# Half-product aggregations and moved edge weights in a graph attention layer

## The chip, the cores and the metric

The kernel runs on one core of a Trainium2 chip. It computes a whole graph network of four layers in one launch, in 32-bit floating point, with its weights in HBM and its activations in SBUF. The metric is the device time of one launch in microseconds (us); the median of three runs is what is compared.

A core has five engines with queues of their own, each of which takes its instructions in order: TensorE multiplies matrices (PE in the profile; PEld is its loading of the stationary operand), VectorE (DVE), ScalarE (ACT) and GpSimd (POOL) do elementwise work, and SyncE (SP) issues the transfers (DMAs). An engine waits for another through semaphores.

## The reference

There are 512 nodes with 768 features and 16384 edges. The change is in the graph attention of layer 0, which has eight heads in its first part and one in its second:

```
def gat_layer(x, W, a_s, a_d, b, edge_index, concat):
    h = (x @ W).reshape(n, H, C)                       # H = 8, C = 768
    alpha_s = jnp.einsum('nhc,hc->nh', h, a_s)         # score of a node as source
    alpha_d = jnp.einsum('nhc,hc->nh', h, a_d)         # and as target
    e = jax.nn.leaky_relu(alpha_s[src] + alpha_d[dst], NEG_SLOPE)
    m = jax.ops.segment_max(e, dst, num_segments=n)
    e = jnp.exp(e - m[dst])
    denom = jax.ops.segment_sum(e, dst, num_segments=n)
    alpha = e / (denom[dst] + EPS)
    out = jax.ops.segment_sum(h[src] * alpha[:, :, None], dst, num_segments=n)
    return out.reshape(n, H * C) + b

h = jax.nn.elu(gat_layer(x, W1, a_src1, a_dst1, b1, edge_list, concat=True))
out = gat_layer(h, W2, a_src2, a_dst2, b2, edge_list, concat=True)
```

So for each head i: h_i = x W1_i (512x768 by 768x768), edge weights alpha (as a dense 512x512 matrix w, target by source, since the graph is small), g_i = elu(w h_i + b), and h2 += g_i W2_i.

## The kernel before, in words

**Counts.** `edge_counts` builds a dense matrix `cnt` of how many edges lead from each source to each target, and from it `off`, which is 0 where an edge exists and 1e30 where none does (L725). The weights of a head come from the two scores of each node (`node_scores`, L796: four multiply-and-sum instructions of 128x768 for a score) in `weighing` (L737 to L763): TensorE turns the source scores into a row (L329), VectorE takes row minus `off` with its maximum (L743), three tiny steps make the negative maximum (L745 to L748), ScalarE adds the target score (L753), VectorE applies the slope of 0.2 (L754), ScalarE the exp (L755), VectorE multiplies by `cnt` and sums (L756), and scales (L763). Each of these is done for four tiles of 128 targets by 512 sources. `turned` (L783) transposes w into wT, source by target, on TensorE, 16 blocks of 128x128.

**Products.** Products of 768x768 matrices are made in seven half-products instead of eight (the Strassen-Winograd scheme). `SplitA` (L395) prepares four sums of quarters of the activations, `SplitB` (L429) four differences of quarters of the weights, on GpSimd, in place for one of them (L438 to L441: three times four instructions of 128x384 for a weight matrix). `strassen` (L498) makes a product whose output is either feature-major or token-major, and adds the half-products up on VectorE: `u2` at L551, `u3` at L554, then L555, L560 and L564. `strassen_add` (L593) makes a product that is added into a running sum; each half-product is added as it comes (`add`, for h2 at L921), so that one half-product can be added to two or three places. Within a column or row group, `first` and `second` are staged so that the second part of a group is written after the first part of the next (`staged`, L491).

**The order.** The loop at the end of the `gat0` block runs over i = 0 to 8. In step i it makes head i's products h_i (`heads`, the heads stage), then aggregates head i-1 (`aggregate`, L898: for each of six feature chunks four products of 128x128 by 128x512, then elu, and the sums for the projection on GpSimd), then makes head i's edge weights (`edge_weights`), and then projects head i-1 through W2 (`project`). The transposes of head i-1's weights are steps that a background list feeds into head i's products, one for each half-product (`tick`, L465). For head 0 the edge weights are in that list too. Instructions of such a step are pinned behind the last one of each engine (`pinned`). Beyond this a scheduler at build time sets the order in each engine's queue, so that instructions of neighbouring stages interleave a little.

**Weights from HBM.** Two buffers take turns: W1_i in one, W2_i in the other, each loaded in three pieces of 768 KB (`split_weights`). A load begins when the last product that reads the old contents of its buffer has ended, and each piece's GpSimd differences follow as it lands.

Of the kernel before, what the change touches and what calls it, by code (L numbers as in the profile page):

```python
# [18 lines left out]
P = 128  # L19
# [78 lines left out]
def kernel(ctx: ExitStack, tc: tile.TileContext, a: dict, out: bass.AP):  # L98
# [296 lines left out]
    class SplitA:  # L395


        def __init__(self, xT, eng, ready=True):
            h = KC // 2
            self.st = big_tile("sx")[:, : 4 * h * HT].rearrange("p (i k n) -> p i k n", i=4, k=h)  # L400
            self.eng = eng
            self.a11, self.a12 = xT[:, :h, :HT], xT[:, h:, :HT]
            self.a21, self.a22 = xT[:, :h, HT:], xT[:, h:, HT:]
            self.s = [None] + [self.st[:, i] for i in range(4)]
            if ready:
                self.all_sums()
# [18 lines left out]
    def ready(src):  # L425

        return SplitB(split_weights(src))

    class SplitB:  # L429


        def __init__(self, w):
            h = KC // 2
            tt = diff_tile("tw").rearrange("p (i k n) -> p i k n", i=3, k=h)
            b11, b12 = w[:, :h, :HC], w[:, :h, HC:]
            b21, b22 = w[:, h:, :HC], w[:, h:, HC:]
            for k in range(h):
                G.tensor_sub(tt[:, 0, k], b22[:, k], b12[:, k])  # L438
                G.tensor_sub(b12[:, k], b12[:, k], b11[:, k])  # L439
                G.tensor_sub(tt[:, 1, k], b22[:, k], b12[:, k])  # L440
                G.tensor_sub(tt[:, 2, k], b21[:, k], tt[:, 1, k])  # L441
            self.b11, self.b21, self.b22 = b11, b21, b22
            self.t = [None, b12, tt[:, 1], tt[:, 0], tt[:, 2]]

# [53 lines left out]
    def strassen(A, B, use, feature, then=None, extra=None, fresh=False):  # L498
# [6 lines left out]
        def product(bank, a, b, c, start, stop):  # L505
            tick()
            for k in range(KC // 2):
                if feature:
                    l, r = b[:, k, ts(c, P)], a[:, k, :]
                else:  # L510
                    l, r = a[:, k, ts(c, P)], b[:, k, :]
                T.matmul(bank, l, r, start=start and k == 0, stop=stop and k == KC // 2 - 1,  # L512
                         skip_group_check=True)
# [78 lines left out]

    def strassen_add(A, B, add, then=None):  # L593

# [42 lines left out]
        def chunk(m):  # L637
            def first():
                if m == 0:
                    plain()  # L640
                add(2 + m, 1, product(m, "z", A.s[1], B.t[1], True))
                add(m, 1, product(m, "y", A.s[2], B.t[2], True))
                add(2 + m, 1, product(m, "y", A.s[3], B.t[3], False))

            def second():
                add(m, 1, product(m, "z", A.s[4], B.b22, False))
                add(2 + m, 0, product(m, "y", A.a22, B.t[4], False))

            return first, second
# [11 lines left out]
    cnt = gone.tile([P, NT, N], FP, name="cnt")  # L661
    off = gone.tile([P, NT, N], BF, name="off")
    cnt_dram = tc.dram_tile([P, NT, N], FP, name="cnt_dram")
# [6 lines left out]
    def edge_counts(gp):  # L670
# [24 lines left out]
        for g in range(n_groups):  # L695
# [15 lines left out]
            for u in range(2):  # L711
# [6 lines left out]
                else:  # L718
# [4 lines left out]
                    G.tensor_add(low, low, r)  # L723
        for t in range(NT):
            S.activation(off[:, t, :], cnt[:, t, :], AF.Relu, bias=bigc, scale=-BIG)  # L725
        nc.sync.dma_start(cnt_dram, cnt)
# [9 lines left out]

    def weighing(w, src4, dst4, cnt, off):  # L737

        srow = row_of(src4)
        yield  # L740
        mx = tiny(NT, name="ga_mx")
        for t in range(NT):
            V.tensor_tensor_reduce(w[:, t, :], srow, off[:, t, :], 1.0, -3.0e38,  # L743
                                   ALU.subtract, ALU.max, mx[:, t : t + 1])
# [22 lines left out]

    def edge_weights(src4, dst4, gp, cnt, off):
        w = weight_tile(gp)
        for _ in weighing(w, src4, dst4, cnt, off):  # L770
            pass
        return w
# [33 lines left out]

    def last_gat(h, as_row, ad_row, gp, cnt, off, between=None):

        s4, d4 = node_scores(h, row(as_row), gp), node_scores(h, row(ad_row), gp)
        ew = edge_weights(s4, d4, gp, cnt, off)  # L810
        made = between() if between else None
        wT = by_source(ew, gp)
        token_product(by_chunk(wT), lambda s: h[:, s, :], add_to_x)
        return made
# [7 lines left out]
    def heads(i):  # L822
        B = first_two.pop(0) if first_two else head_weights(i)
        h = token_major("h")
        strassen_token(xs, B, lambda t, c, ps: S.copy(h[:, t, ts(c, HC)], ps), None,
                       None if i else n0.rest)
        flush()
        return h, node_scores(h, row(f"g0_as{i}"), gp), node_scores(h, row(f"g0_ad{i}"), gp)

    with tc.tile_pool(name="graph", bufs=1) as gp:  # L830
# [15 lines left out]
        loose.append(background[0])  # L846
        head0 = heads(0)
        drain()
# [46 lines left out]
    with tc.tile_pool(name="gat0", bufs=2) as gp:  # L895
        h2 = token_major("h2")

        def aggregate(i, h, wT, norm=None):  # L898
            gT = feature_major("gT")
            sums = SplitA(gT, G, False)  # L900
            for n, f in enumerate((0, 3, 1, 4, 2, 5)):
                ps = psum()
                for s in range(NT):
                    T.matmul(ps, h[:, s, ts(f, P)], wT[:, s, :], start=s == 0, stop=s == NT - 1)  # L904
                elu(gT[:, f, :], ps, col("g0_b1", i * KC + f))
                if norm and n < NT:
                    norm.chunk(n)
                if f >= KC // 2:
                    sums.sums(f - KC // 2)
            return sums  # L910

        def project(i, sums):
# [9 lines left out]

            strassen_add(sums, ready(a["L0_gnn_W2"][i * D : (i + 1) * D, :]), add)
            flush()
# [4 lines left out]
        def degrees():  # L929
# [9 lines left out]
            V.tensor_mul(dinv, dinv, nw)  # L939

        done = None
        for i in range(9):
            if done:
                g, hg, ew = done
                wT = gp.tile([P, NT, N], FP, tag="edge_wT", name="edge_wT", bufs=wt_bufs[0])
                if i < 8:
                    if i == 1:
                        background.append(delayed(5, weighing(ew, s4, d4, cnt, off)))
                    background.append(delayed(0 if i == 1 else 8, turned(ew, wT)))
                else:  # L950
                    for _ in turned(ew, wT):
                        pass
            if i < 8:
                h, s4, d4 = heads(i) if i else head0
                drain()
            if done:
                norm = performer_norm() if i == 8 else None
                sums = aggregate(g, hg, wT, norm)
            if i < 8:
                done = i, h, edge_weights(s4, d4, gp, cnt, off) if i else weight_tile(gp)  # L960
            else:
# [5 lines left out]
        x = load_x()  # L967
        qT = last_gat(h2, "g0_as", "g0_ad", gp, cnt, off, lambda: performer_features(ys, 0))
        add_row_to(x, row("g0_b2"))
# [1086 lines left out]
```

## Time and profile before

| | us |
|---|---|
| median of three runs (lowest to highest) | 3091.04 (3089.36 to 3091.62) |
| the profiled execution | 3090.54 |
| its span, first to last instruction | 3088.8 |
| TensorE busy | 3004.2 |
| layer 0's eight heads, from the first product of head 1 to the end of the last aggregation | 117.7 to 691.5 |
| one head in the middle: heads stage, aggregation, projection | 29.2, 20.6, 28.5 |
| TensorE's waits at the six projections from head 0 on | 1.19, then 1.10 each |

A row of the timeline reads: start in us from the span's start, duration, engine, line, operation, output and inputs with their shape and how many instructions are merged, and in brackets how long the engine had been idle before and what ended it. A 32-bit product is two matmul instructions. Matmul instructions are pipelined: the record of one of 128x384 lasts 487 ns, but they start 0.32 us apart. The rows of "stretches" give for a window its length, each engine's busy time and count, and then the granted clock of TensorE (1.00 is full), the busy share of the DMA engines and GB/s.

### The profile page before, as it was taken

The page shows a single profiled execution, that of the slowest core. Times are in us where ns is not written, and L with a number is a line of the kernel's source. Part 1 is how long each engine was busy: PE and PEld are TensorE (multiplying, and loading weights), DVE is VectorE, ACT ScalarE, POOL GpSimd, SP SyncE. Part 2 cuts the span into 40 slices and gives each one's busy share as a digit, 9 for nine tenths or more (in the row PEclk, how much of TensorE's full clock was granted, in tenths as well). Part 3 has the DMA queues.
Part 4 walks back from the last instruction along what each step waited for, and adds up shares of the span by engine and source line. Part 5 has one row for each costly group of instructions (what it writes and reads, how often), then busy time and mean ns, then how long its engine had stood idle before and what let it go on. Part 6 is the DMA issues. An engine that isn't in the chain of part 4 may idle for free.

```text
span 3088.8 us, 31610 instructions
## 1 busy us (share of the span) xinstructions
PE 3004.2 (97%) x11757; PEld 2006.4 (65%) x11757; DVE 1481.0 (48%) x3416; ACT 753.1 (24%) x1436; POOL 1430.7 (46%) x1532
## 2 busy tenths in 40 slices
PE   7999999999999999999899999999999999999989
PEld 3555555556766767765675367877777776677755
DVE  9855444555255235456766436333333335462341
ACT  7432322251352112004432213100000012221111
POOL 4344444452506553645641434455544457355610
PEclk9999999999999999999999999999999999999999
DMA  3211111222203223322112412122222223122222
GB/s 116 89 63 64 65 64 69 72 92 82 82 1 118 77 87 118 111 75 80 38 72 63 148 67 98 67 92 93 92 92 78 77 92 123 67 83 82 99 75 62
DMA packets 92691, 253.63 MB, mean 82 GB/s; under 512 B 9889, under 2 KB 14881, under 8 KB 91514
## 3 DMA queue, kind: packets, MB, share of 16 engines
q1 hardware_dynamic: 92538, 251.61, 23.5%
q8 instruction: 93, 1.52, 0.2%
q14 instruction: 60, 0.49, 0.1%
HBM read 244.23 MB, written 7.36 MB: 81 GB/s over the span
## 4 chain that ended last, share of the span: by engine, by line
PE 87%; DVE 9%; POOL 2%; ACT 1%; issue 1%; DMA 0%; SPq 0%; POOLq 0%; ACTq 0%; DVEq 0%
PE ps L512 43%; PE ps L605 23%; PE ps L904 5%; PE ps L308 4%; DVE oh L705 1%; PE ps L1112 1%; PE ps L1099 1%; PE ps L298 1%; PE ps L274 1%; PE ps L1937 1%; PE ps L1600 1%; POOL room L1458 1%; DVE edge_w L754 1%; PE ps L708 1%; DVE edge_w L743 1%
## 5 line engine op out<-in xcount | busy, mean ns | idle before, releaser
L438 POOL TENSOR_TENSOR tw<-w 128x384 f32<-128x384 f32 x246 | 247.3, 1015 | 960.0 <-DMA w<-in_L_gnn_W 341.8
L512 PE MATMUL ps<-sx,w 128*128 128x256 f32 x1188 | 317.3, 381 | 2.9 <-DVE sx L420 2.6
L512 PE MATMUL ps<-sx,tw 128*128 128x256 f32 x1188 | 290.3, 381 | 0.4
L605 PE MATMUL ps<-w,sx 128*128 128x384 f32 x720 | 256.5, 487 | 4.2 <-DVE sx L420 2.9
L440 POOL TENSOR_TENSOR tw<-w 128x384 f32<-128x384 f32 x246 | 252.2, 1032 | 9.6
L441 POOL TENSOR_TENSOR tw<-w,tw 128x384 f32<-128x384 f32 x246 | 250.4, 1025 | 10.4
L439 POOL TENSOR_TENSOR w<-w 128x384 f32<-128x384 f32 x246 | 250.8, 1028 | 8.9
L605 PE MATMUL ps<-tw,sx 128*128 128x384 f32 x720 | 250.4, 487 | 0.0
L512 PEld LDWEIGHTS ps<-sx,w 128*128 128x128 f32 x1188 | 225.6, 191 | 37.9 <-PE ps L512 2.2
L512 PEld LDWEIGHTS ps<-sx,tw 128*128 128x128 f32 x1188 | 219.9, 190 | 42.7 <-DVE st_u L551 7.2
L527 ACT COPY st_p<-ps 128x256 f32<-128x256 f32 (+1 forms) x127 | 49.9, 394 | 720.4 <-PE ps L512 681.5
L551 DVE TENSOR_TENSOR st_u<-st_p,ps 128x256 f32<-128x256 f32 (+1 forms) x127 | 57.2, 450 | 338.0 <-PE ps L512 337.9
L605 PEld LDWEIGHTS ps<-tw,sx 128*128 128x128 f32 x720 | 136.3, 190 | 94.6 <-DVE x L1821 1.2
L605 PEld LDWEIGHTS ps<-w,sx 128*128 128x128 f32 x720 | 136.6, 190 | 94.1 <-POOL tw L441 4.1
L654 DVE TENSOR_TENSOR x<-x,ps 128x384 f32<-128x384 f32 x216 | 115.2, 552 | 164.7 <-PE ps L605 163.4
L512 PE MATMUL ps<-xfT,w 128*128 128x256 f32 x720 | 176.9, 380 | 0.2
L512 PE MATMUL ps<-w,sx 128*128 128x384 f32 x456 | 169.2, 492 | 1.8 <-DVE ps L555 1.8
L904 PE MATMUL ps<-edge_wT,h 128*128 128x512 f32 x384 | 166.1, 593 | 0.0
L512 PE MATMUL ps<-tw,sx 128*128 128x384 f32 x456 | 160.4, 488 | 4.7 <-DVE st_u L551 4.2
L554 DVE TENSOR_TENSOR st_u<-st_p,ps 128x256 f32<-128x256 f32 (+1 forms) x127 | 57.2, 450 | 203.2 <-PE ps L512 203.2
L512 PEld LDWEIGHTS ps<-xfT,w 128*128 128x128 f32 x720 | 136.2, 190 | 23.9 <-issue 1.3
L605 PE MATMUL ps<-w,hid 128*128 128x384 f32 x432 | 142.9, 488 | 0.0
(485 smaller groups left out, 5067.6 us busy)
## 6 DMA issues: line engine op xcount, KB each, us to landing
w<-in_L_gnn_W SPq DMA_DIRECT2D x60, 768.0 KB, 6.8
w<-in_L_mix_fc_w SPq DMA_DIRECT2D x48, 768.0 KB, 6.2
row<-in_rows SPq DMA_DIRECT2D x39, 384.0 KB, 4.5
w<-in_L_mix_qkv_w SPq DMA_DIRECT2D x18, 768.0 KB, 5.2
w<-in_L_ffn_w SPq DMA_DIRECT2D x18, 768.0 KB, 7.1
w<-in_L_ffn_routed_gate SPq DMA_DIRECT2D x18, 768.0 KB, 6.0
w<-in_L_ffn_routed_up SPq DMA_DIRECT2D x18, 768.0 KB, 6.6
w<-in_L_ffn_routed_down SPq DMA_DIRECT2D x18, 768.0 KB, 5.7
```

The costliest lines, as they stand in the source:

```text
L308: T.matmul(ps, parts[k][:, ts(t, P)], w_of(k)[:, ts(c, HC)], start=k == 0, stop=k == n - 1)
L438: G.tensor_sub(tt[:, 0, k], b22[:, k], b12[:, k])
L439: G.tensor_sub(b12[:, k], b12[:, k], b11[:, k])
L440: G.tensor_sub(tt[:, 1, k], b22[:, k], b12[:, k])
L441: G.tensor_sub(tt[:, 2, k], b21[:, k], tt[:, 1, k])
L512: T.matmul(bank, l, r, start=start and k == 0, stop=stop and k == KC // 2 - 1, skip_group_check=True)
L527: S.copy(b["p1"], b["x"])
L551: V.tensor_add(b["u2"], b["p1r"], b["y"])
L554: V.tensor_add(u3, b["p1r"], b["y"])
L605: T.matmul(b[name], l[:, k, ts(m, P)], r[:, k, :], start=start and k == 0, stop=k == KC // 2 - 1, skip_group_check=True)
L654: V.tensor_add(x[:, t, ts(j, HC)], x[:, t, ts(j, HC)], ps)
L904: T.matmul(ps, h[:, s, ts(f, P)], wT[:, s, :], start=s == 0, stop=s == NT - 1)
```

## The change

Three things are changed, all in layer 0's graph attention.

1. The aggregation of a head is made by `strassen_feature`, in seven half-products of 256x384 quarters, in place of the plain product. For it h_{i-1} goes through `SplitB` (GpSimd, eight instructions, in place, with two small tiles and a new one, `h_diff`, for the results) and wT through `SplitA` (VectorE, four instructions of 128x512).
2. The edge weights of heads 0 to 6 become steps in the next head's products (`splitting`, which holds the differences, the weights, the transposes and the sums). The target scores are computed after the aggregation (`target_scores`), since the differences overwrite h. `off` is no longer kept: each weighing makes it anew into the weight tile, in four ScalarE instructions. Head 7's weights stay beside projection 6, and its transposes become steps there.
3. The projection's `strassen_add` gets `raw=True`: the two half-products of `A.a22` with `B.t[4]`, which need no sums of activations, come at the start, in banks of their own, and are added apart.

```diff
-        def __init__(self, xT, eng, ready=True):
-            h = KC // 2
-            self.st = big_tile("sx")[:, : 4 * h * HT].rearrange("p (i k n) -> p i k n", i=4, k=h)
+        def __init__(self, xT, eng, ready=True, st=None):
+            h = self.h = xT.shape[1] // 2
+            if st is None:
+                st = big_tile("sx")[:, : 4 * h * HT]
+            self.st = st.rearrange("p (i k n) -> p i k n", i=4, k=h)
...
-        def __init__(self, w):
-            h = KC // 2
-            tt = diff_tile("tw").rearrange("p (i k n) -> p i k n", i=3, k=h)
+        def __init__(self, w, tt=None):
+            h = w.shape[1] // 2
+            if tt is None:
+                tt = diff_tile("tw").rearrange("p (i k n) -> p i k n", i=3, k=h)
+                tt = [tt[:, i] for i in range(3)]
...
-    def strassen_add(A, B, add, then=None):
+    def strassen_add(A, B, add, then=None, raw=False):
...
                 if m == 0:
                     plain()
+                    for n in range(2 * raw):
+                        add(2 + n, 0, product(n, "p4", A.a22, B.t[4], True))
                 add(2 + m, 1, product(m, "z", A.s[1], B.t[1], True))
                 add(m, 1, product(m, "y", A.s[2], B.t[2], True))
-                add(2 + m, 1, product(m, "y", A.s[3], B.t[3], False))
+                ps = product(m, "y", A.s[3], B.t[3], False)
+                add(2 + m, 1, ps)
+                if raw:
+                    add(2 + m, 0, ps)
             def second():
                 add(m, 1, product(m, "z", A.s[4], B.b22, False))
-                add(2 + m, 0, product(m, "y", A.a22, B.t[4], False))
+                if not raw:
+                    add(2 + m, 0, product(m, "y", A.a22, B.t[4], False))
...
-        for t in range(NT):
-            S.activation(off[:, t, :], cnt[:, t, :], AF.Relu, bias=bigc, scale=-BIG)
...
-    def weighing(w, src4, dst4, cnt, off):
+    def weighing(w, src4, dst4, cnt):
         srow = row_of(src4)
+        for t in range(NT):
+            S.activation(w[:, t, :], cnt[:, t, :], AF.Relu, bias=bigc, scale=-BIG)
         yield
         mx = tiny(NT, name="ga_mx")
         for t in range(NT):
-            V.tensor_tensor_reduce(w[:, t, :], srow, off[:, t, :], 1.0, -3.0e38,
+            V.tensor_tensor_reduce(w[:, t, :], srow, w[:, t, :], 1.0, -3.0e38,
                                    ALU.subtract, ALU.max, mx[:, t : t + 1])
...
-        return h, node_scores(h, row(f"g0_as{i}"), gp), node_scores(h, row(f"g0_ad{i}"), gp)
+        return h, node_scores(h, row(f"g0_as{i}"), gp)
+
+    def target_scores(i, h):
+        return node_scores(h, row(f"g0_ad{i}"), gp)
...
+        last_sums = []
+
+        def splitting(w, wT, h, both, s4=None, d4=None):
+            tt = gp.tile([P, 2, NT // 2, HC], FP, tag="h_diff", name="h_diff", bufs=1)
+            at = len(nc.cur_bb.bb.instructions)
+            both.append(SplitB(h, [Chunks([part_tile("p1r", HC) for _ in range(2)]), tt[:, 0], tt[:, 1]]))
...
+            yield
+            if s4 is not None:
+                yield from weighing(w, s4, d4, cnt)
+                yield
+                yield
+            yield from turned(w, wT)
+            both.append(SplitA(wT, V, True, weight_tile(gp).rearrange("p t n -> p (t n)")))
+
-        def aggregate(i, h, wT, norm=None):
+        def aggregate(i, hB, wA, norm=None):
             gT = feature_major("gT")
             sums = SplitA(gT, G, False)
-            for n, f in enumerate((0, 3, 1, 4, 2, 5)):
-                ps = psum()
-                for s in range(NT):
-                    T.matmul(ps, h[:, s, ts(f, P)], wT[:, s, :], start=s == 0, stop=s == NT - 1)
-                elu(gT[:, f, :], ps, col("g0_b1", i * KC + f))
...
+            def use(c, n, j, ps):
+                f = 3 * j + c
+                elu(gT[:, f, ts(n, HT)], ps, col("g0_b1", i * KC + f))
+
+            def then(c):
+                sums.sums(c)
...
+            strassen_feature(wA, hB, use, then)
+            flush()
...
-            strassen_add(sums, ready(a["L0_gnn_W2"][i * D : (i + 1) * D, :]), add)
+            strassen_add(sums, ready(a["L0_gnn_W2"][i * D : (i + 1) * D, :]), add, None, True)
...
         for i in range(9):
...
+            if 0 < i < 8:
+                both, steps = parts_of(*done)
+                background.append(delayed(4, steps) if i == 1 else steps)
+                h, s4 = heads(i)
+            elif i == 0:
+                h, s4, d4 = head0
+            drain()
+            if i:
                 norm = performer_norm() if i == 8 else None
-                sums = aggregate(g, hg, wT, norm)
-            if i < 8:
-                done = i, h, edge_weights(s4, d4, gp, cnt, off) if i else weight_tile(gp)
+                g, sums = i - 1, aggregate(i - 1, *both, norm)
+            if 0 < i < 8:
+                d4 = pinned(lambda: target_scores(i, h))
+            if i < 7:
+                done = i, h, weight_tile(gp), s4, d4
+            elif i == 7:
+                both, steps = parts_of(i, h, edge_weights(s4, d4, gp, cnt))
+                background.append(delayed(8, steps))
             else:
                 ys, va = performer_values(norm)
```

`parts_of` makes the wT tile and calls `splitting`. In the part left out of `splitting`, the differences of h are put on GpSimd's queue behind the last sums of the aggregation before.

## The prediction

> **What bounds the kernel now.** I read the page first: the row of busy times and the chain that ended last.
>
> ```profile
> PE 3004.2 (97%) x11757; PEld 2006.4 (65%) x11757; DVE 1481.0 (48%) x3416; ACT 753.1 (24%) x1436; POOL 1430.7 (46%) x1532
> ...
> PE 87%; DVE 9%; POOL 2%; ACT 1%; issue 1%; DMA 0%; SPq 0%; POOLq 0%; ACTq 0%; DVEq 0%
> ```
>
> TensorE is the chain. A change pays by the products it removes and costs by each time TensorE has to wait. The change lies in layer 0's attention, so next I read TensorE's timeline over one head.
>
> ```profile
> 275.88 2.10 PE L512 MATMUL ps<-w,xnT 128*128 128x384 f32 x6
> ...
> 305.11 20.76 PE L904 MATMUL ps<-edge_wT,h 128*128 128x512 f32 x48
> ...
> 326.14 4.04 PE L605 MATMUL ps<-w,gT 128*128 128x384 f32 x12
> ...
> 337.73 2.20 PE L605 MATMUL ps<-w,gT 128*128 128x384 f32 x6 [1.10 <-DVE h L921]
> ...
> 354.61 2.10 PE L512 MATMUL ps<-w,xnT 128*128 128x384 f32 x6
> ```
>
> A head takes 354.61 - 275.88 = 78.73 us: 29.2 for the next head's products (heads stage), 20.6 for the aggregation, 28.5 for the projection. Its only wait is 1.10 us, where additions (L921) stand behind the edge weights on VectorE. A 384-wide matmul instruction costs 0.3225 us (six in 1.935) and a product has two, so 0.645. From two starts of 256-wide ones (761.54 - 758.95, 12 instructions) I take 0.216 us each.
>
> ```profile
> 758.95 2.75 PE L512 MATMUL ps<-sx,tw 128*128 128x256 f32 x12
> ...
> 761.54 1.03 PE L512 MATMUL ps<-yT,w 128*128 128x256 f32 x4
> ```
>
> **Aggregations.** Before: 48 instructions, 20.6 us. After: seven half-products x 3 column groups x 2 blocks x 2 = 84 instructions of 0.216, 18.1. Eight heads: -19.8 us. Added beside them: VectorE gets four sums of wT (0.6 each), 15 evacuations (0.42) and twelve half-width last steps of elu instead of six; ScalarE gets 36 half-width steps instead of 18 plus three copies; GpSimd gets eight differences of h (1.0 each). ScalarE per third: the 384- and 256-wide copies of L527 take 0.48 and 0.37, so a 256-wide step of elu is near 0.42, and 12 x 0.42 + 0.37 = 5.4 us under 6.05 us of TensorE. That is hidden, with little over. The differences of h run on GpSimd in the projection, after its sums, where it was idle (24.7 us in the row for 279.16 below). The wT sums end close to their first reader; I allow 0.3 us a head, +2.4.
>
> **Projections.** The three products without sums now give 18 products x 0.645 = 11.6 us before the first one with sums, and the last sums end near 10 us; this covers them. The waits of before go: 1.19, five of 1.10 and 0.75, -7.4. In their place the target scores (four of L796) stand between the additions that TensorE waits for. They meet GpSimd's sums, as explained next; walking the additions I get 0.7 us a head, six heads, +4.2. Two more additions each are hidden.
>
> **Edge weights as steps in the next head's products.** This decides. The old place was beside the projection, where GpSimd is mostly idle. The new place is the heads stage, where GpSimd splits the next W2.
>
> ```profile
> 279.16 0.99 POOL L438 TENSOR_TENSOR tw<-w 128x384 f32<-128x384 f32 x1 [24.74 <-DMA w<-in_L_gnn_W]
> ...
> 290.75 0.99 POOL L441 TENSOR_TENSOR tw<-w,tw 128x384 f32<-128x384 f32 x1
> ```
>
> Twelve instructions back to back, from 3.3 to 15.9 us of the stage. After the change they begin later: W2's load waits for the last reader of the old W2, which was two products before the projection's end and is now its very last product, so with the 4.9 us from release to first split seen here they begin at 5.2 us. What happens when VectorE's edge-weight steps meet them is seen once in the trace of before, at head 0, whose weights already ran in the background:
>
> ```profile
> 132.50 0.86 DVE L748 TENSOR_SCALAR ga_nm<-ga_nm 128x4 f32<-128x4 f32 x1
> ...
> 133.41 0.99 POOL L440 TENSOR_TENSOR tw<-w 128x384 f32<-128x384 f32 x1
> ...
> 134.08 2.27 DVE L754 SCALAR_TENSOR_TENSOR edge_w<-edge_w 128x512 f32<-128x512 f32 x2 [0.72 <-ACT edge_w L753]
> ...
> 134.48 1.32 POOL L441 TENSOR_TENSOR tw<-w,tw 128x384 f32<-128x384 f32 x1
> ```
>
> A four-element step takes 0.86 us instead of 0.17, ending with GpSimd's instruction; two L754 take 2.27 instead of 1.3, and GpSimd's instruction grows to 1.32. The two engines take turns, instruction by instruction, when VectorE's operands lie all in SBUF. L796 shows the same (0.95 alone, 1.74 beside GpSimd); rows with a PSUM operand (L551, L805, L743) don't change. So each L745, L748, L754, L756 pays up to 1 us, and a 512-wide one takes 1.4 instead of 0.6. L763 is seen only without GpSimd (0.42); a like one, L719, goes from 0.43 to 0.95, so I let it take turns too.
>
> Now the walk, in the order of the built program, from the stage's first product (0). TensorE turns the score row at 2.4. ScalarE makes the 'off' term there (four of about 0.65, after its copy at 2.6), so the four maxima end at 5.9. **Without GpSimd**: three tiny steps to 6.4; L754 twice, exp on ScalarE, L756 twice to 9.1; the addition u2; the other two tiles to 12.2; the addition u3; the scaling (L763) to 15.4. TensorE needs u2 at 9.5, u3 at 12.2 and the scaled weights, for the transposes, at 14.6: about 0.9 us of waits. **Taking turns**: tiny steps to 7.3; L754 at 8.9 and 10.3; L756 at 11.8 and 13.3; u2 at 13.9, so TensorE waits 4.4 us; L754 at 14.8 and 16.2; L756 at 17.7 and 19.2; u3 at 19.7, TensorE waits another 3.3; scaling from 21.2 to 22.8. The transposes start at 22.9 instead of 14.6: +8.3. Check by total: 12 splits x 0.93 = 11.2, less 2.6 that fit beside maxima and additions, is 8.6 more than the 15.4. Bounds: 0.9 where nothing meets, 9.5 where nothing overlaps. I take 8.2, because the trace shows the turns. Five heads stages (2, 4, 5, 6, 7) have this order: +41. Stage 3 has u2 first and its transposes later: +5.5. Stage 1 has the transposes at its end: +2 (0 to 5). Together +48.5.
>
> **The clock.** One wait of this kind is in the trace, and what follows it:
>
> ```profile
> 117.72 3.69 PE L512 MATMUL ps<-w,xnT 128*128 128x384 f32 x6 [2.19 <-ACT st_p L527]
> ...
> 115.00:120.00 5.00, 2.81 (x7) 1.24 (x6) 4.67 (x10) 1.88 (x4) 0.41 (x1) 0.83 0.75 232
> ```
>
> After 2.19 us of idling six instructions take 3.69 us instead of 2.1, and the granted clock over 115 to 120 us is 0.83. The Trainium skill (TensorE: Matmul & The Clock Gate, section HAM oscillation) warns of idle gaps above about 3.4 us. By that rule only the 4.4 us wait costs clock, and the half-speed work after it hides before u3: about 0. By the row a gap of 2.2 us already does, and the 1.1 us ones do not; then the second wait of 3.3 counts too, and its slow stretch falls on work that nothing hides, up to 1.7 us. I go by the row: 1.5 us in six stages, +9.0.
>
> **The rest.** Head 7's weights stay beside projection 6, but its target scores come into the same queue, all ahead of the additions: four L796 and four maxima, then L754 and L756, in turns with GpSimd's sums and differences. The third addition comes near 21 us; TensorE has products until 12. +9 (3 alone, 11 in full turns). After aggregation 7 the elu has less cover: +1. The 'off' steps leave ScalarE's queue at the end of head 0's products, where TensorE waited 2.19: -2. The same steps in each stage are on ScalarE, in the walk above. Extra rows and weights are not loaded; later layers are unchanged.
>
> **Sum:** -19.8 + 2.4 - 7.4 + 4.2 + 48.5 + 9.0 + 9 + 1 - 2 = +44.9 us. The profiled execution took 3090.5 (span 3088.8 and 1.7 around it), the median is 3091.0; the same difference on the median gives 3136.
>
> **Rivals.** (1) *Faster.* The turns stay short, because W2's pieces land later or the weights run ahead of them, and the stages wait 0.9 us: -19.8 + 2.4 - 7.4 + 4.2 + 7 x 0.9 + 2 + 1 - 2 = -13, so 3078. For it: TensorE has 14 us of products before it needs the transposes. Against it: the splits start at 5.2 and the steps at 5.9. All but the stages 2 to 7 sums to about -10.6, so a wait of 1.8 us a stage decides the sign. (2) *Half the turns.* Splits and steps meet for about half, 4 us a stage and no slow clock: -10.6 + 24 = +13, 3104. (3) *ScalarE paces the aggregation.* If elu's dependent half-width steps take 0.5 us instead of 0.42, a third takes 6.4 instead of 6.05: +0.35 x 3 x 8 = +8 on top, 3144. For it: each step waits for the one before. Against it: the 512-wide ones follow each other at 0.60 to 0.66. That the change does not do what it says can be left out: the built order has the 84 instructions and the steps where the diff puts them.
>
> **How the numbers follow.** The main case 0.68 (own range 3118 to 3152), rival 1 0.10, rival 2 0.13, rival 3 0.09. The range of 3097 to 3156 leaves out rival 1 and the outer ends. Runs of this kernel tell about 0.2% (6 us) from no change. Faster by more than that: rival 1, 0.10. Within it: the upper edge of rival 1 and lower edge of rival 2, 0.05. Slower: 0.85.
>
> **What would show it.** Right: in the heads stages waits of TensorE for VectorE's u2, u3 and scaling, some 8 us together, with L754's and L756's successors at 1.4 us while GpSimd splits; stretches of granted clock under 1.0 there; aggregations of 18 to 19 us; no wait at the first product with sums. Wrong: GpSimd's splits outside 5 to 20 us of the stage, or steps at 0.6 us beside them; then rival 1. Aggregations near 20 us would mean rival 3.

## The result

The changed kernel takes 3135.23 us (3133.74 to 3136.26 in four runs) beside 3091.01 us (3089.36 to 3091.62) for the kernel before: ratio 1.0145, 95% interval 1.0133 to 1.0157, 44 us slower. The prediction was 3136. The total agrees better than its parts do, as the stages show.

The page of the profiled execution (3135.01 us, span 3133.1, 44.3 more than the span before) has these rows of busy times and of the chain that ended last:

```profile
PE 3010.1 (96%) x12039; PEld 2067.9 (66%) x12045; DVE 1596.8 (51%) x3632; ACT 791.8 (25%) x1632; POOL 1520.9 (49%) x1596
...
PE 84%; DVE 10%; ACT 3%; POOL 2%; issue 1%; DMA 0%; SPq 0%; another core or an unknown queue 0%; POOLq 0%; ACTq 0%; DVEq 0%
```

TensorE's part of the chain fell from 87 to 84%, ScalarE's rose from 1 to 3, VectorE's from 9 to 10: TensorE now waits for chains of small steps. Below is TensorE's timeline over one head's step: heads stage 4, aggregation 3 and projection 3. (Stages are numbered by their head.)

```profile
367.69 2.10 PE L525 MATMUL ps<-w,xnT 128*128 128x384 f32 x6
...
380.14 2.99 PE L525 MATMUL ps<-tw,sx 128*128 128x384 f32 x6 [2.82 <-DVE st_u L564]
...
385.76 0.91 PE L525 MATMUL ps<-tw,xnT 128*128 128x384 f32 x2 [1.34 <-DVE st_u L567]
...
388.57 1.52 PE L806 MATMUL ps<-ident,edge_w 128*128 128x128 f32 x4
...
404.15 1.03 PE L525 MATMUL ps<-edge_wT,h 128*128 128x256 f32 x4
...
422.42 4.03 PE L619 MATMUL ps<-w,gT 128*128 128x384 f32 x12
...
449.70 2.10 PE L525 MATMUL ps<-w,xnT 128*128 128x384 f32 x6
```

The step is 449.70 - 367.69 = 82.0 us, before it was 78.7. The heads stage grew from 29.2 to 36.5 us, the aggregation fell from 21.0 (with the row transposes ahead of the next stage) to 18.3, the projection from 28.5 to 27.3, with no wait. What VectorE and GpSimd did in the stage that grew:

```profile
373.94 0.86 DVE L767 TENSOR_SCALAR ga_nm<-ga_nm 128x4 f32<-128x4 f32 x1
374.72 2.08 DVE L773 SCALAR_TENSOR_TENSOR edge_w<-edge_w 128x512 f32<-128x512 f32 x2
376.73 1.48 DVE L775 SCALAR_TENSOR_TENSOR edge_w<-edge_w,cnt 128x512 f32<-128x512 f32 x1
...
379.55 0.54 DVE L564 TENSOR_TENSOR st_u<-st_p,ps 128x384 f32<-128x384 f32 x1
...
385.16 0.54 DVE L567 TENSOR_TENSOR st_u<-st_p,ps 128x384 f32<-128x384 f32 x1
```

```profile
372.69 1.00 POOL L451 TENSOR_TENSOR tw<-w 128x384 f32<-128x384 f32 x1 [13.62 <-DMA w<-in_L_gnn_W]
...
376.34 1.33 POOL L454 TENSOR_TENSOR tw<-w,tw 128x384 f32<-128x384 f32 x1
...
387.24 1.00 POOL L454 TENSOR_TENSOR tw<-w,tw 128x384 f32<-128x384 f32 x1
```

The twelve splits of W2 begin 5.0 us into the stage and end at 20.6. L775 takes 1.48 us beside them and a four-element step (L767) 0.86. u2 (L564) and u3 (L567), which stand behind such steps, end 12.4 and 18.0 us into the stage. TensorE's products behind the first wait run at about half speed (2.99 us where six usually take 2.10).

TensorE's longest wait in the eight heads is at projection 6, which still has head 7's edge weights beside it:

```profile
691.15 6.24 PE L619 MATMUL ps<-w,gT 128*128 128x384 f32 x12 [10.18 <-DVE h L971]
```

All of layer 0's attention, from the starts of its stages in TensorE's two timelines:

| part | predicted | measured |
|---|---|---|
| heads stages 2 to 7 | +41 + 5.5 + clock 9 = +55.5 | +39.7 |
| products of heads 0 and 1, aggregation 0 | -2.2 | +10.0 |
| aggregations 1 to 6 | -13.1 | -13.9 |
| projections 0 to 5 | -6.6 + 4.2 = -2.4 | -7.5 |
| projection 6 | +8.3 | +11.5 |
| aggregation 7, next layer's values, projection 7 | -1.2 | +2.1 |
| everything later | 0 | about +2.5 |

Aggregation 2 overlaps heads stage 3; I count it like its neighbours and the rest to the stage. The row transposes (0.43 us a head) moved from the aggregation into the heads stage, and are left out of both. Two terms are far off, with opposite signs: the heads stages by 16 us, the start with head 0 by 12. The first experiments ask what the heads stages' 40 us are, and what the start's 10 are.

### The profile page after: what moved, and what is told of

Same layout as the page of the kernel before. It is cut to its first block, busy times and chain, and to the rows that moved or that the text cites. A ratio compares the mean times of both kernels' runs of the same rounds, so it can differ in the third digit from the quotient of the medians.

```text
span 3133.1 us, 32709 instructions
## 1 busy us (share of the span) xinstructions
PE 3010.1 (96%) x12039; PEld 2067.9 (66%) x12045; DVE 1596.8 (51%) x3632; ACT 791.8 (25%) x1632; POOL 1520.9 (49%) x1596
## 4 chain that ended last, share of the span: by engine, by line
PE 84%; DVE 10%; ACT 3%; POOL 2%; issue 1%; DMA 0%; SPq 0%; another core or an unknown queue 0%; POOLq 0%; ACTq 0%; DVEq 0%
PE ps L525 44%; PE ps L619 25%; PE ps L308 4%; DVE edge_w L775 1%; PE ps L1167 1%; DVE edge_w L773 1%; PE ps L1154 1%; PE ps L298 1%; PE ps L274 1%; PE ps L1992 1%; PE ps L1655 1%; POOL room L1513 1%; PE ps L727 1%; DVE st_u L815 1%; DVE edge_w L762 1%
## 5 line engine op out<-in xcount | busy, mean ns | idle before, releaser
L619 PE MATMUL ps<-tw,sx 128*128 128x384 f32 x720 | 250.5, 487 | 0.0
L540 ACT COPY st_p<-ps 128x256 f32<-128x256 f32 (+1 forms) x151 | 58.9, 391 | 737.3 <-PE ps L525 698.4
L564 DVE TENSOR_TENSOR st_u<-st_p,ps 128x256 f32<-128x256 f32 (+1 forms) x151 | 67.2, 445 | 276.1 <-PE ps L525 274.4
L619 PEld LDWEIGHTS ps<-tw,sx 128*128 128x128 f32 x720 | 136.0, 190 | 94.6 <-DVE x L1876 1.2
L525 PE MATMUL ps<-tw,sx 128*128 128x384 f32 x456 | 171.3, 513 | 26.7 <-DVE st_u L564 26.1
L567 DVE TENSOR_TENSOR st_u<-st_p,ps 128x256 f32<-128x256 f32 (+1 forms) x151 | 67.2, 445 | 210.0 <-PE ps L525 209.8
L525 PEld LDWEIGHTS ps<-tw,sx 128*128 128x128 f32 x456 | 88.0, 198 | 89.9 <-DVE st_u L564 34.3
```

The costliest lines, as they stand in the source:

```text
L540: S.copy(b["p1"], b["x"])
L564: V.tensor_add(b["u2"], b["p1r"], b["y"])
L567: V.tensor_add(u3, b["p1r"], b["y"])
L619: T.matmul(b[name], l[:, k, ts(m, P)], r[:, k, :], start=start and k == 0, stop=k == KC // 2 - 1, skip_group_check=True)
```

## The experiments

Line numbers in experiments differ by a few to some thirty from those of the changed kernel. The code is shortened; `...` and comments stand for what is left out. `-` and `+` lines are against the changed kernel unless said otherwise. Differences in us are ratios to the kernel before, times 3090.

**Splits of W2 behind the weights** (`splits_later`).

```
         yield from weighing(w, s4, d4, cnt)
+        go = tiny(NT, name="ga_go")
+        G.tensor_sub(go, w[:, NT - 1, :NT], w[:, NT - 1, :NT])
+        scaled.append(nc.cur_bb.bb.instructions[-1].name)
...
-    strassen_add(sums, ready(W2), add, None, True)
+    B = ready(W2)          # each GpSimd instruction of it queued behind scaled[-1]
+    strassen_add(sums, B, add, None, True)
```

> The changed kernel, with one thing moved: GpSimd's twelve splits of the next W2 are queued behind a four-element subtraction that reads the last scaled edge weights (one extra GpSimd instruction per head), so that they can no longer meet the weighing steps. Theory 1 (VectorE and GpSimd take turns, and that is what the heads stages lose): L773 and L775 fall from 1.4 to about 0.65 us, TensorE waits for u2 and u3 for 1 us at most, no half-clock stretch follows; stages 2 and 4 to 7 fall from 36.5 to about 30, stage 3 by some 4.5; 6.2 x 5 + 4.5 = 36 less, perhaps 2 given back where the splits now meet the sums of wT: 3099 to 3102 us. Theory 2 (the chain of dependent steps standing ahead of u2 and u3 in VectorE's queue costs it, whatever GpSimd does): the stages stay near 36, 3130 to 3136 us.

Measured: 3106.18 us, ratio 1.0052 (1.0037 to 1.0067): 29 us less than the change. Stages 2 and 4 to 7 take 30.1 us each. VectorE's rows in stage 4 (which begins at 361.93 here), then TensorE's:

```profile
368.24 1.28 DVE L773 SCALAR_TENSOR_TENSOR edge_w<-edge_w 128x512 f32<-128x512 f32 x2
369.71 0.69 DVE L775 SCALAR_TENSOR_TENSOR edge_w<-edge_w,cnt 128x512 f32<-128x512 f32 x1 [0.19 <-ACT edge_w L774]
...
370.94 0.55 DVE L564 TENSOR_TENSOR st_u<-st_p,ps 128x384 f32<-128x384 f32 x1
...
387.57 1.27 DVE L422 TENSOR_TENSOR edge_w<-edge_wT 128x512 f32<-128x512 f32 x1
388.76 1.49 DVE L424 TENSOR_TENSOR edge_w<-edge_wT 128x512 f32<-128x512 f32 x1
```

```profile
374.72 0.91 PE L525 MATMUL ps<-tw,xnT 128*128 128x384 f32 x2 [0.32 <-DVE st_u L567]
...
397.74 1.13 PE L525 MATMUL ps<-edge_w,st_p1r 128*128 128x256 f32 x4 [1.20 <-DVE st_u L564]
```

L775 is back at 0.69 us, u2 ends 9.6 us into the stage instead of 12.4, TensorE waits 0.32 us. The chain of steps ahead of u2 and u3 is the same, only GpSimd is elsewhere: theory 1 holds. By the two traces 25.6 of the 29 us lie ahead of projection 6; the rest comes later, in code that is the same in both, and is taken up below. The second pair of VectorE's rows shows what is given back: the splits now end at 389.7 and slow two of the sums of wT (1.27 and 1.49 against 0.68), the source scores behind them run late, and TensorE waits 1.20 us in the aggregation, which grows by 1.5. I had allowed 2 us in all for that; it is 1.5 a head, some 9 us for six heads, which accounts for the distance to the expected 3099 to 3102.

**Plain products in the aggregations** (`steps_plain`).

```
-    both.append(SplitB(h, ...))        # eight differences of h on GpSimd
+    both.append(h)
...
-    both.append(SplitA(wT, V, True, ...))
+    both.append(wT)
...
-    strassen_feature(wA, hB, use, then)
+    for n, f in enumerate((0, 3, 1, 4, 2, 5)):
+        ...                            # four products of 128x128 by 128x512, elu, sums, as before
```

> The changed kernel with the aggregations as plain products again (48 matmul instructions of 512 columns a head), so without the sums of wT and without GpSimd's differences of h; edge weights as steps and the projections stay as changed. If the half-products are worth what their instructions say (2.76 us a head by the two traces) and nothing else: 8 x 2.76 = 22 more, 3157. My expectation takes off what their preparation costs elsewhere: GpSimd's differences of h no longer slow head 0's target scores (the 5.6 us wait at the end of head 0's products), the aggregation of head 0 starts without its 4.3 us wait, and in projection 6 GpSimd only has the sums (-4): 3157 - 5 - 4 - 4 = 3144. If the heads stages change by more than 1 us, the turns with W2's splits are not what slows them.

Measured: 3129.52 us, ratio 1.0131 (1.0114 to 1.0148). I had expected 3144. Without half-products the change is no slower; by the two profiled spans (3128.1 and 3133.1) it is 5 us faster. The heads stages stay (36.5 to 37.2), so they owe nothing to the half-products. Aggregations 1 and 3 to 6 rise by 2.3 us each, 14 for six. But at the two ends more is won than I took off: the products of heads 0 and 1 -6.2, aggregation 0 -4.1, projection 6 -9.1, aggregation 7 with the values behind it -2.0: 21 us where I had taken off 13. The rows of the changed kernel at head 0, VectorE's and then TensorE's, show why:

```profile
118.31 1.74 DVE L815 SCALAR_TENSOR_TENSOR st_u<-h,row 128x768 bf16<-128x768 f32 x1
...
126.65 0.54 DVE L564 TENSOR_TENSOR st_u<-st_p,ps 128x384 f32<-128x384 f32 x1
...
155.23 1.55 DVE L815 SCALAR_TENSOR_TENSOR st_u<-h,row 128x768 bf16<-128x768 f32 x1
...
156.72 0.68 DVE L207 COPY edge_wT<-ps 128x512 f32<-128x512 f32 x1
```

```profile
127.24 4.21 PE L525 MATMUL ps<-tw,sx 128*128 128x384 f32 x6 [5.61 <-DVE st_u L564]
...
157.45 1.22 PE L525 MATMUL ps<-edge_wT,h 128*128 128x256 f32 x2 [3.20 <-DVE edge_wT L207]
```

Head 0's scores (L815) stand ahead of u2, and most take 1.74 us each in turns with GpSimd's differences of h, which the change put there; in `steps_plain`, without these differences, most take 0.95 and TensorE waits 0.89 us for u2 instead of 5.61. Head 1's source scores then stand ahead of the last copy into wT (L207), again in turns, with splits of a W. The waits of aggregation 0 are 4.8 us in the change and 0.9 here.

**Edge weights beside the projection again** (`old_place`).

```
-        d4 = pinned(lambda: target_scores(i, h))
-    if i < 7:
-        done = i, h, weight_tile(gp), s4, d4
-    elif i == 7:
-        ...
+    if i < 8:
+        done = (i, h, edge_weights(s4, d4, gp, cnt)) if i else (0, h, weight_tile(gp), s4, d4)
```

> The changed kernel with the edge weights of heads 1 to 7 beside the projection again, made in one go there, and both scores right behind the head's products, as before; half-products and projections as changed. The buffer of the edge weights now holds the sums of wT until the aggregation's end, so the weights can't begin before that; each projection should look like projection 6 of the changed kernel, which waits 10.2 us, less some 4.3 for the target scores that no longer stand in between. Theory 1: heads stages 2 to 7 fall to 29 (-42 in all), projections 0 to 5 rise by 9.8 each (+59), projection 6 falls by 4, 3 for scores in the aggregation: about 3150 (3130 to 3165). Rival (the old place was nearly free and would be so again, 1.1 us of wait): 3135 - 42 - 10 = about 3080.

Measured: 3134.81 us, ratio 1.0146 (1.0131 to 1.0161): as slow as the change, by another way. The heads stages are 29.2, but projections 0 to 6 take 32.6 to 34.4, aggregations 20.9 and aggregation 0 32.4. Projections rise by 5.4 each and not by 9.8, so the expected 3150 is missed: most wait 4.8 us, in three pieces, where projection 6 of the change waits 10.2 in one. The rival falls too: with the half-products the old place isn't free. The reason that I gave, the sums of wT in the buffer of the weights, explains little of it: in the kernel before the maxima begin only after the aggregation too. The next rows are VectorE's and GpSimd's in projection 3 here, and then VectorE's same step in projection 2 of the kernel before.

```profile
444.74 1.48 DVE L775 SCALAR_TENSOR_TENSOR edge_w<-edge_w,cnt 128x512 f32<-128x512 f32 x1
...
444.22 2.85 POOL L452 TENSOR_TENSOR h<-h 128x384 f32<-128x384 f32 x2
```

```profile
333.62 0.68 DVE L756 SCALAR_TENSOR_TENSOR edge_w<-edge_w,cnt 128x512 f32<-128x512 f32 x1
```

The last maximum ends 6.0 us into the projection here, behind the four 'off' steps on ScalarE, and 3.4 us into it before. The steps that follow then meet the half-products' own differences of h on GpSimd, in turns again. What each of the two costs, and what a buffer of their own for the sums of wT would change, was not tried.

**The early products undone** (`no_raw`), and **the early products alone** (`before_early`, against the kernel before).

```
-    strassen_add(sums, ready(W2), add, None, True)
+    strassen_add(sums, ready(W2), add)
```

> The changed kernel with the projection's two products of a22 back at their old place, so only four products without sums come first. If the early products are what covers the sums of gT (they end 10.2 us into the projection, and four products cover 7.7): 2.3 us of wait in six projections, 14 more, 3149. By the single sums in the trace the product that follows needs only the first sum (6.6 us in) and the next one the third (9.4 us in, needed at 9.7): no wait, and the part does nothing: 3133 to 3138. I hold the second.

> The kernel before, with the projection's two products of a22 made early as in the change and nothing else: the part of the change that is free. The waits of the projections (1.19, five of 1.10, 0.75) are for additions behind the edge weights on VectorE, over at 10.5 us of the projection; six products without sums and one with sums last 11.6 to 13: 7 less than before, 3083. Rival: with more products ahead of them the additions are needed by as many banks sooner, and the wait only moves: 3089 to 3092.

Measured: `no_raw` 3137.27 us, ratio 1.0153 (1.0137 to 1.0168), which can't be told from the change, as I had expected of the total. `before_early` 3091.44 us, ratio 1.0006 (0.9998 to 1.0014), no gain, against my expectation. A projection's TensorE rows of each:

```profile
433.98 0.91 PE L619 MATMUL ps<-w,sx 128*128 128x384 f32 x2 [1.26 <-POOL sx L412]
```

```profile
403.87 4.04 PE L605 MATMUL ps<-w,gT 128*128 128x384 f32 x12
407.74 4.03 PE L605 MATMUL ps<-tw,gT 128*128 128x384 f32 x12
...
415.45 2.20 PE L605 MATMUL ps<-w,gT 128*128 128x384 f32 x6 [1.09 <-DVE h L927]
```

Without the early products four projections wait 1.26 us for GpSimd's sums and one 2.38 us, against my expectation of no wait. Projections 0 to 5 take 9.7 us more than in the change. The total hides this: the heads stages are 2.0 us shorter together, and by the two traces the rest of it, 4 us, is made up from projection 6 on.

With the early products alone, the old 1.09 us remains. The product that waits goes on in the first product's bank, which VectorE's additions must have read, and in VectorE's queue these additions stand behind the edge weights. The products that now come first only take the places of others ahead of it. So the projections' gain needs both: the weights gone from VectorE's queue, and the early products against the sums.

**A filled wait** (`filled_wait`).

```
     V.tensor_add(b["u2"], b["p1r"], b["y"])
+    if filling and not feature and c == 0:     # heads 2 to 7
+        idle = psum()[:, :n]
+        for _ in range(4):
+            T.matmul(idle, A.s[2][:, 0, ts(c, P)], B.t[2][:, 0, :], start=True, stop=True)  # pinned in place
```

> The changed kernel with four idle products (eight matmul instructions of 384 columns, 2.6 us, into a bank that nobody reads) put where TensorE waits for u2 in the heads stages of heads 2 to 7; extra work, nothing left out. The wait then is under 2 us, and the traces show no half-clock stretch after such a wait in this stage. If the clock costs what the prediction's clock step says (1.5 us a stage): 9 less, 3126. If the half-speed products only use up the second wait, for u3, which ends when VectorE gets there: the second wait grows by what the first loses and nothing is won, 3133 to 3137. I hold the second.

Measured: 3137.9 us, ratio 1.0158 (1.0144 to 1.0172). The change's stage 4 by stretches of 5 us (TensorE's granted clock stands ahead of the last two numbers), and then the same stage here, which begins 2.4 us later:

```profile
375.00:380.00 5.00, 2.33 (x8) 1.05 (x6) 5.00 (x7) 2.67 (x4) 4.84 (x4) 1.00 0.13 50
380.00:385.00 5.00, 4.27 (x8) 1.88 (x8) 5.00 (x6) 1.92 (x3) 4.76 (x5) 0.66 0.00 0
385.00:390.00 5.00, 4.04 (x13) 2.09 (x14) 4.60 (x10) 0.96 (x2) 3.08 (x3) 1.00 0.00 0
```

```profile
380.00:385.00 5.00, 3.45 (x12) 1.78 (x11) 5.00 (x8) 2.05 (x4) 4.76 (x5) 1.00 0.00 0
385.00:390.00 5.00, 2.91 (x9) 1.25 (x8) 4.90 (x9) 1.43 (x3) 4.76 (x5) 1.00 0.00 0
```

The wait for u2 is 1.55 us instead of 2.82, the clock stays at 1.00 throughout, and the stage takes 36.48 us beside 36.45. The second wait took up what the clock gave: it is 2.09 us where it was 1.34. Stage 7 stays clean too, 36.46 us beside 36.64. In stages 2, 5 and 6 a half-clock stretch came all the same, behind the second wait of 2.08 us or a longer first one of 2.35, and these are 0.5 to 1.7 us longer; stage 3, which overlaps an aggregation, is 2.2 us longer with it. So in the stages that stayed clean the clock was free, as I held; where half-speed products fall behind the last wait it isn't.

**Both repairs** (`both_fixes`): `splits_later`, and plain products as in `steps_plain` where `i in (0, 7)`.

> The changed kernel with GpSimd's W2 splits behind the scaled weights (as in splits_later) and with plain products in the aggregations of heads 0 and 7, so that no differences of h run on GpSimd beside head 0's target scores and beside head 7's edge weights; half-products for heads 1 to 6. From splits_later (3106.2) minus what steps_plain showed at the two ends: head 0's products 6.3, aggregation 0 4 to 6, projection 6 9.0, aggregation 7 0.3, the wait ahead of the next layer's values 1.7: 21 to 23 less, 3083 to 3085 us. If the two losses have one cause in common (GpSimd's load as a whole), the two savings don't add up: 3095 or more.

Measured: 3086.07 us, ratio 0.9990 (0.9982 to 0.9998). The two savings add up (19 to 20 us below `splits_later`, 21 to 23 expected), and the sum is just below the kernel before. A head's step is 30.1 + 19.7 + 27.3 = 77.1 us, before 78.7.

**How much of it is half-products** (`later_plain`): `splits_later` with all aggregations plain.

> splits_later with plain products in the aggregations of all heads: what is left of the change without half-products. Per head 30.1 for the heads stage, 20.6 for the aggregation, 27.2 for the projection: 77.9, where both_fixes has 77.1 and the kernel before 78.7. If so, half-products are worth 0.8 us a head here and not 2.8: 3086 + 6 x 0.8 = 3091.

Measured: 3089.25 us, ratio 0.9995 (0.9987 to 1.0004), with the stages as expected (30.1, 20.6, 27.2). A half-product aggregation is 2.3 us shorter on TensorE alone (18.3 against 20.6) and 0.9 us with what it meets.

**The scores elsewhere**, both from `both_fixes`: four in a row behind the aggregation's first third (`fixes_scores`), and one to every third half-product (`spread_scores`).

```
     def then(c):                           # fixes_scores
         sums.sums(c)
+        if c == 0 and between:
+            got.append(pinned(between))    # node_scores of the next head
...
+    background.append(delayed(5, scoring(s4, h, row(f"g0_as{i}"), 3)))   # spread_scores
+    if i == 7:
+        background.append(scoring(d4, h, row(f"g0_ad{i}"), 1))
```

> both_fixes, with the source scores of the next head moved from right behind its products to behind the first third of the aggregation. In splits_later TensorE waits 1.2 us in each of six aggregations for u2, which stands behind these four multiply-and-sums on VectorE: 7 less than both_fixes, about 3077. Rival: there they meet GpSimd's splits of W1 and hold up the elu and the additions of the second third instead: no gain, 3083 or more.

> both_fixes (3086.1), with the source scores of heads 2 to 7 dealt out one multiply-and-sum to every third half-product of the aggregation, from the sixth on, and head 7's target scores one to each of the next, instead of four in a row behind the heads' products and behind the aggregation. In fixes_scores the four in a row, in turns with GpSimd, held up u2 and u3 of the last third and four steps of ScalarE behind them. Dealt out they fit beside 1.2 us of VectorE's work per three half-products (2.6 us): the 1.2 to 1.4 us of wait in six aggregations go (-7), and projection 6 loses some 4 of its 4.7 us wait: 3075 to 3079. If VectorE has no room for them even so: 3084 to 3090.

Measured: 3091.58 us, ratio 1.0008 (0.9999 to 1.0016), and 3089.25 us, ratio 0.9997 (0.9989 to 1.0005). Neither gains, and both of my expectations failed. The wait at the aggregation's start goes or shrinks, and others come behind it (in `fixes_scores` 0.2 to 0.7 us each, for u2 and u3 of the last third); a step takes some 77.6 and 77.2 us. Projection 6 still waits some 5 us. Perhaps VectorE has no room there; this was not tested.

**Head 7's target scores back in their old place** (`three_plain`, `three_later`): from `both_fixes`, plain products also in aggregation 6, and

```
     s4 = node_scores(h, row(f"g0_as{i}"), gp)
+    if i == 7:
+        d7.append(node_scores(h, row(f"g0_ad{i}"), gp))
```

> both_fixes (3086.1) with head 7's target scores right behind its source scores again, as before the change, instead of between projection 6 and its edge weights, and with a plain product in aggregation 6 too, so that the four more multiply-and-sums hold up no u2 there. Aggregation 6 goes from 20.2 to 21.0, projection 6 from 35.9 to 30 or 31 (it waited 0.75 before the change, and the 'off' steps and GpSimd's sums add a little): 4 to 5 less, 3081 to 3083 us. If it is not the target scores that make projection 6 wait 4.7 us, it stays at 36: 3087.

> three_plain with one omission of it mended: there head 6's plain branch did not queue the splits of W2 behind head 6's scaled weights, so that they met the weighing steps in the last heads stage, which took 36.5 us as in the changed kernel, while the other stages took 30.1. Projection 6 did fall, from 35.9 to 30.7. With the splits queued in that stage too: 30.1 there, 6.3 less than three_plain's 3091.2, 3083 to 3086 us; if the meeting in one stage is not what costs it 6.3, it stays near 3091.

Measured: `three_plain` 3091.18 us, ratio 1.0005 (0.9997 to 1.0013). Projection 6 fell as expected, from 35.9 to 30.7, but heads stage 7 took 36.5: in head 6's branch W2's splits were not queued behind the weights. The fall is not the target scores' alone. In `steps_plain` and `later_plain` these are where the change put them, all aggregations are plain, and projection 6 takes 32.4 us. So most of the fall goes with the plain aggregation 6, and 1 to 2 us with the scores.

With the splits queued there too, `three_later` takes 3084.35 us (3083.0 to 3086.7), ratio 0.9983 (0.9974 to 0.9992), with stage 7 at 30.1. Like `both_fixes` it lies below the kernel before by more than the interval, and it does so by 5 us. VectorE's first row of L775 in that stage, of the one and of the other:

```profile
591.38 1.48 DVE L775 SCALAR_TENSOR_TENSOR edge_w<-edge_w,cnt 128x512 f32<-128x512 f32 x1
```

```profile
589.63 0.69 DVE L775 SCALAR_TENSOR_TENSOR edge_w<-edge_w,cnt 128x512 f32<-128x512 f32 x1 [0.19 <-ACT edge_w L774]
```

One stage with turns and without, 36.5 and 30.1, in otherwise equal kernels: this is the cleanest measurement of the price.

## Why the prediction came true, step by step

**Edge weights as steps in the next head's products: right in mechanism, some 15% too dear, and this term decided.** The turns are shown: 29 us came back when only GpSimd's place changed. The walk held well: splits at 5.0 us of the stage (5.2 predicted), maxima over at 5.8 (5.9), u2 at 12.4 (13.9), u3 at 18.0 (19.7), scaling over at 22.0 (22.8). By the end of the first two L773 it was 1.2 us too long; they took 2.08 together where I had let both take a full turn. All stages together measure 39.7 us where the walk alone had 46.5: per stage 7.3, or 6.8 without the row transposes, for 8.2. The turns themselves are 6.3 of it (36.5 to 30.1), the rest is there without them. The Trainium skill (SBUF — State Buffer, section "Who interferes with whom") has the rule behind it: a VectorE instruction with two SBUF inputs and a GpSimd instruction that reads SBUF exclude each other for the whole instruction. The rows agree: L775 1.48 and 0.69, while u2, with one input in PSUM, takes 0.54 and 0.55.

**The clock: wrong, +9 for about 0.** By the row of before I was right that waits below 3.4 us can bring the half clock (2.82 us did, at 0.66 over the next stretch), and right that slow products behind the first wait hide: the second wait ends when VectorE gets to u3, so they only shorten it. What failed is the second wait. I put it at 3.3 us, with a slow stretch behind it on work that nothing hides. In stages 4 to 7 it was 1.07 to 1.34 us, since u3 came earlier than in my walk and the slow products had used up the rest, and the clock behind it was 1.00. The price itself was about right: in `filled_wait` the second waits of 2.08 us in stages 2 and 6 did bring a slow stretch, and these two stages are 1.2 and 1.6 us longer.

**Aggregations: right, 18.3 us where 18.1 were worked out, and without the 0.3 us allowed for late sums.** Rival 3, ScalarE pacing, is out: TensorE waits in none of aggregations 1 to 6.

**The start: wrong, -2 for +10.** The failed step is the sentence that the differences of h "run on GpSimd in the projection, after its sums, where it was idle". That holds for heads 1 to 6. Head 0 has no projection ahead of it: its differences start at once and meet its eight score instructions, and u2 waits for them 5.6 us. I had put 2 us on stage 1 for its late transposes alone. Plain products at head 0 took 10 us back.

**Projections: better than predicted, -7.5 for -2.4, with the wrong reason for part of it.** I put the end of the old waits down to the early products. Alone these do nothing. The target scores cost nothing beside them: I had priced them at 4.2 us.

**Projection 6: right in kind, +11.5 for +8.3.** All that I named stands in the queue. From the change to `both_fixes`, without GpSimd's differences of h beside it, the projection falls by 5.5 us. It falls by 4.7 more in `three_later`, and most of that goes with the plain aggregation 6, which I had not named.

**Everything later: +2.5 instead of nothing, and this is scatter.** The products of this part are the same in all fourteen traces, and from projection 7's first product to the last one of the kernel they take 2362.3 to 2368.2 us; before has 2364.5 and the change 2367.2. TensorE's waits there add up to 50.0 and 49.3 us. What differs more is the half-clock work: by the starts of the products it costs about 20.6 us in the shortest of these parts and 25.8 in the longest. So differences of 3 us between single traces, the last 3 of `splits_later` too, say nothing of the change.

So the forecast had the deciding mechanism and its size to some 15%. With the clock, 16 us too much there, and 5 on the projections, were made up by 12 too little at the start and 9 at the end: that the total is right to 1 us is luck. Rivals 1 and 2 needed shorter turns and are out: the heads stages took 39.7 us more, where they had some 6 and 24.

## What to carry to other kernels

Work moved from a busy queue to an "idle" one must be looked up against every engine that shares something with its new neighbours: here VectorE's steps were moved from beside a mostly idle GpSimd to beside twelve GpSimd instructions, and many of them doubled. Moving them back did not help, since the change had put GpSimd work there as well. The repair was to queue the other engine's work behind them, with one four-element instruction that reads the last result. And a loop's first and last turns need their own walk: together they cost about as much here (10 and 14 us) as three heads of the middle.

## What the hardware showed that I had not expected

Whether a wait of about 2.1 us brings the half clock is not settled by its length. At the end of head 0's products TensorE waits 2.19 us in the kernel before and 2.18 in `before_early`: the six instructions that follow take 3.69 us in the one and 2.20 in the other. Over layer 0's attention in all traces (100 to 800 us), counting a stretch of at least 1 us in which matmuls follow each other at 1.7 to 2.3 times their usual distance and which begins within 3.2 us of the wait's end: waits of 0.9 to 2.0 us had one in 5 of 85 cases, 2.0 to 2.3 us in 9 of 19, 2.3 to 3 us in 10 of 13, longer ones in all 26. In `filled_wait` the same wait, 2.08 and 2.09 us, had one in two stages and none in two others. What sets the difference stays open. The prediction weighed the Trainium skill's rule of about 3.4 us (TensorE: Matmul & The Clock Gate, section HAM oscillation); for this kernel it is too generous, and the measurement decides.
